# A two-layer graph transformer on one core: layer 1's table weights loaded beside the experts, and a last table tile cut to the nodes' rows

## The chip, the cores and the metric

The kernel runs on one core of a Trainium2 chip. The metric is the device time in microseconds; a shorter time is better. Five engines work from queues of their own: PE (matmul, with its weight loads PEld), DVE (vector), ACT (scalar functions), POOL and SP. In this kernel SP only issues DMAs, and POOL only issues DMAs that gather or scatter rows. All DMAs share the core's 16 DMA engines.

## The reference, cut to what matters

The inputs are 3,125 nodes of 256 features and 100,000 edges with one of 8 types. Two layers follow one another; each adds a graph part, a mixing part and an expert part to the nodes.

```python
xn = _layernorm(x, axis=-1)
x = x + _L0_gnn_ref(xn, edge_index, ...) + _L0_mix_ref(xn[None], ...)[0]
x = x + _L0_ffn_ref(_layernorm(x, axis=-1)[None], ...)[0]        # 8 experts, the best 2 per node
xn = _layernorm(x, axis=-1)
x = x + _L1_gnn_ref(xn, L1_gnn_W, ..., edge_type_8) + _L1_mix_ref(xn[None], ...)[0]
x = x + _L1_ffn_ref(_layernorm(x, axis=-1)[None], ...)[0]
```

What lies around the change is the end of layer 0 and the start of layer 1's graph part:

```python
out = (weights[:, :, None] * sel).sum(axis=1)                    # layer 0: two experts' results per node
...
h_all = jnp.einsum('nf,rof->rno', x, W).reshape(r, n, h, d)      # layer 1: 8 types x 3125 nodes x 256
h_src = h_all[edge_type, src]                                    # one row per edge
scores = einsum(h_src, attn_src) + einsum(h_dst, attn_dst)       # then a softmax over each node's edges
out = jax.ops.segment_sum(h_src * w[..., None], dst, num_segments=n)
```

The layer-1 mixing part needs k and v of all nodes (with a norm of their own), their product kv, and the weights wq, wk, wv, wo and bo.

## The kernel before, in words

The nodes are padded to 25 tiles of 128 (`NB = 25`, `NP = 3200`). The last tile holds only `LAST = 53` nodes; the other 75 of its rows belong to no node. The node features stay on the chip in `xs`.

**The experts (layer 0).** `experts` runs 32 steps of 256 rows (8 fixed, 24 by a plan), over which `s` counts. A step loads the rows (`fx`), small vectors and two halves of an expert's weights (`fw1`, `fw2`, 1 MB each) on SP, two steps of buffers ahead; PE makes the hidden values (`fhp`, line 2068), ACT their Gelu, PE the results (`fyp`, line 2076), DVE adds a bias, and ACT's queue stores the result to `route_y` in DRAM (line 2079). Then `beside(s)` is called, which places other small work next to the step: block lists for layer 1, and the attention's score weights at steps 16 and 22. Here PE, DVE and ACT run in the written order (`manual_schedule` with `ORDERED`); the order of SP and POOL is found by the framework's scheduler, except for what `keep_in_program_order` marks.

**The table stage (layer 1).** After the experts come ten weight loads on SP (lines 353 and 2321 to 2328: `wq`, `wo`, `wt`, `wkv`, `bo`, `kg`, `kb`), and then a loop over the 25 tiles. For a tile POOL gathers the two expert results of each node from `route_y` (`y0`, `y1`, three buffers each, line 2342), DVE adds them to `xs` and takes the norm, PE transposes (`xt1`), and PE multiplies with `wt` for all 8 types (`hp`, line 2362), with `score_w` for the attention's terms (`ap`) and with `wkv` for k and v (`kvp`). ACT and DVE copy the results to `stage`, and SP stores the stage into the table `tab2` in DRAM (line 2375):

```python
rows = tab2[:R * NP, :].rearrange("(r t p) c -> t p r c", r=R, p=P)
...
nc.sync.dma_start(rows[t], stage)         # 128 partitions x 8 types x 264 floats (1,056 bytes a piece)
```

SP also stores the tile's own attention terms (`apart`) and its transposed features (`x1t`). In this loop the scheduler orders all engines.

**The attention blocks (layer 1).** `Layer1.run` is in written order again. POOL gathers one table row per edge, 128 at a time, into the buffers `r` (nine buffers of seven gathers, line 1403); block 0 has 34 of them. A gather reads the whole of `tab2`, so the first waits for every store of it. Beside them SP loads `oe` (line 1207), PE picks each edge's own node terms (`dp`, line 1228), DVE reduces them (`own`, line 1239), and `mix` prepares the mixing weights, before `block` begins with `raw` (line 1422). 25 blocks follow, and out's rows are stored at the end (line 1383; the last store has 53 rows).

Of the kernel before, what the change touches and what calls it, by code (L numbers as in the profile page):

```python
# [8 lines left out]
F32 = mybir.dt.float32  # L9
BF = mybir.dt.bfloat16  # L10
I32 = mybir.dt.int32
AF = mybir.ActivationFunctionType
# [31 lines left out]
def row_bc(v, n, start=0):  # L44

    return bass.AP(tensor=v.tensor, offset=v.offset + start, ap=[[0, P], [1, n]])
# [1962 lines left out]
        nc.vector.tensor_copy(self.back, rank)  # L2009


def experts(tc, C, T, a, pool, wp, wk, ps, beside):

    nc = tc.nc
# [98 lines left out]
def fast(ctx: ExitStack, tc: tile.TileContext, a, out, flag):  # L2113
# [151 lines left out]
    big.close()  # L2265
    late = ctx.enter_context(tc.tile_pool(name="late", bufs=1))


    with tc.tile_pool(name="blk", bufs=1) as blk, tc.tile_pool(name="blk_p", bufs=1, space=PSUM) as blk_p, \
            tc.tile_pool(name="f", bufs=1) as f:  # L2270
        B_ = Blocks(nc, late, dram, blk, a, places)

        score_w = None
        wn = f.tile([P, R, 2, D], F32, name="wn")
# [34 lines left out]
    with tc.tile_pool(name="n1", bufs=1) as n1:  # L2309
        apart = dram.tile([NB, P, 3, HD * R], BF, name="apart")  # L2310
        x1t = dram.tile([(NB + 3) // 4, P, 2, 512], F32, name="x1t")
        cx = n1.tile([P, 2, P], F32, name="cx1")
        wq = load_k(nc, n1, a["L1_mix_wqT"], "wq")
        wo = load_k(nc, n1, a["L1_mix_woT"], "wo")
        with tc.tile_pool(name="r", bufs=1) as r1, tc.tile_pool(name="rw", bufs=3) as rw, \
                tc.tile_pool(name="rc", bufs=1, space=PSUM) as rc, \
                tc.tile_pool(name="rp", bufs=2, space=PSUM) as rp:
# [6 lines left out]
            kg = r1.tile([P, 2, 64], F32, name="kg")  # L2324
            kb = r1.tile([P, 2, 64], F32, name="kb")
            for i, c in enumerate("kv"):
                nc.sync.dma_start(kg[:, i, :], row_bc(a[f"L1_mix_ln_{c}_g"], 64))
                nc.sync.dma_start(kb[:, i, :], row_bc(a[f"L1_mix_ln_{c}_b"], 64))
            pad = r1.tile([1, TW], F32, name="pad")
            nc.vector.memset(pad[:, :D], 0.0)  # L2330
            nc.vector.memset(pad[:, D:], FAR)
            nc.sync.dma_start(tab2[PADTAB:PADTAB + 1, :], pad)

            st = r1.tile([P, NB, 6], F32, name="st_x2")
            mv = r1.tile([P, NB, 2], F32, name="mv_x2")
            rs = r1.tile([P, NB], F32, name="rs_x2")
            cps = [rc.tile([P, P], F32, name=f"kv{g}") for g in range(2)]
            rows = tab2[:R * NP, :].rearrange("(r t p) c -> t p r c", r=R, p=P)
            for t in range(NB):
                for i in range(2):  # L2340
                    y = rw.tile([P, D], F32, name=f"y{i}")
                    nc.gpsimd.indirect_dma_start(  # L2342
                        out=y, out_offset=None, in_=T_.y,
                        in_offset=bass.IndirectOffsetOnAxis(ap=T_.back[:, i * NB + t:i * NB + t + 1], axis=0))
                    nc.vector.scalar_tensor_tensor(xs[:, t, :], y, T_.wt[:, i, t:t + 1], xs[:, t, :],
                                                   op0=OP.mult, op1=OP.add)
                nc.vector.bn_stats(st[:, t, :], xs[:, t, :])
                nc.vector.bn_aggr(mv[:, t, :], st[:, t, :])
                nc.scalar.activation(rs[:, t:t + 1], mv[:, t, 1:2], AF.Sqrt, bias=C.eps)
                nc.vector.reciprocal(rs[:, t:t + 1], rs[:, t:t + 1])  # L2350
                x1 = rw.tile([P, D], F32, name="x1")
                normal(nc, x1, xs[:, t, :], mv, rs, t)
                nc.vector.tensor_add(xs[:, t, :], xs[:, t, :], bo)
                xt = rw.tile([P, 2, P], F32, name="xt1")
                transposed(nc, C, rp, xt, x1)
                nc.sync.dma_start(x1t[t // 4][:, :, t % 4 * P:(t % 4 + 1) * P], xt)

                stage = rw.tile([P, R, TW], F32, name="stage")
                for j in range(R // 2):
                    hp = rp.tile([P, 2, D], F32, name="hp", tag="a")  # L2360
                    for k in range(2):
                        nc.tensor.matmul(hp.rearrange("p r d -> p (r d)"), xt[:, k, :],  # L2362
                                         wt[:, k, j * 512:(j + 1) * 512], start=(k == 0), stop=(k == 1))
                    if j % 2:
                        nc.vector.tensor_copy(stage[:, 2 * j:2 * j + 2, :D], hp)
                    else:
                        nc.scalar.copy(stage[:, 2 * j:2 * j + 2, :D], hp)
                ap = rp.tile([P, 2 * R * HD], F32, name="ap", tag="b")
                for k in range(2):
                    nc.tensor.matmul(ap, xt[:, k, :], score_w[:, k, :], start=(k == 0), stop=(k == 1))  # L2370
                nc.vector.tensor_copy(stage[:, :, D:], ap[:, :R * HD].rearrange("p (r h) -> p r h", r=R))
                a3 = rw.tile([P, 3, HD * R], BF, name="a3")
                bf_parts(nc, rw, a3[:, 0, :], a3[:, 1, :], a3[:, 2, :], ap[:, R * HD:], [P, HD * R])
                nc.sync.dma_start(apart[t], a3)
                nc.sync.dma_start(rows[t], stage)

                n = P if t < NB - 1 else LAST
                kvp = rp.tile([P, 8, 64], F32, name="kvp", tag="b")
                for k in range(2):
                    nc.tensor.matmul(kvp.rearrange("p h d -> p (h d)"), xt[:, k, :], wkv[:, k, :],  # L2380
                                     start=(k == 0), stop=(k == 1))
                mean = rw.tile([P, 8], F32, name="mean")
                nc.vector.tensor_reduce(mean, kvp, AX.X, OP.add)
                nc.vector.tensor_scalar(mean, mean, 1.0 / 64, None, op0=OP.mult)
                kv = rw.tile([P, 8, 64], F32, name="kv")
                nc.vector.tensor_tensor(kv, kvp, mean[:, :, None].to_broadcast([P, 8, 64]), OP.subtract)
                sq = rw.tile([P, 8, 64], F32, name="sq")
                nc.scalar.activation(sq, kv, AF.Square)
                var = rw.tile([P, 8], F32, name="var")
                nc.vector.tensor_reduce(var, sq, AX.X, OP.add)  # L2390
                nc.scalar.activation(var, var, AF.Sqrt, bias=C.eps, scale=1.0 / 64)
                nc.vector.reciprocal(var, var)
                nc.vector.tensor_tensor(kv, kv, var[:, :, None].to_broadcast([P, 8, 64]), OP.mult)
                kv4 = kv.rearrange("p (i h) d -> p i h d", i=2)
                nc.vector.tensor_tensor(kv4, kv4, kg[:, :, None, :].to_broadcast([P, 2, 4, 64]), OP.mult)
                nc.vector.tensor_tensor(kv4, kv4, kb[:, :, None, :].to_broadcast([P, 2, 4, 64]), OP.add)
                kvf = kv.rearrange("p h d -> p (h d)")
                for g in range(2):
                    nc.tensor.matmul(cps[g], kvf[:n, g * P:(g + 1) * P], kvf[:n, D + g * P:D + (g + 1) * P],
                                     start=(t == 0), stop=(t == NB - 1))  # L2400
            for g in range(2):
                nc.vector.scalar_tensor_tensor(cx[:, g, :], cps[g], 1.0 / N, C.blocks[64],
                                               op0=OP.mult, op1=OP.mult)


        with tc.tile_pool(name="at_1", bufs=1) as one, tc.tile_pool(name="at_w", bufs=2) as wk, \
                tc.tile_pool(name="at_r", bufs=9) as rows, tc.tile_pool(name="at_p", bufs=1, space=PSUM) as ps:
            with tc.manual_schedule():
                Layer1(tc, C, a, out, one, wk, rows, ps, B_, tab2, apart, x1t, (cx, wq, wo), xs).run()


@with_exitstack
# [58 lines left out]
```

## Time and profile before

| | |
|---|---|
| median of 3 runs | 3045.12 us (3043.67 to 3058.38) |
| the profiled execution's own time | 3573.77 us |
| its span, from the first instruction to the last | 3571.6 us |
| granted TensorE clock, mean | 0.864 |
| PE, DVE, ACT, POOL busy in the span | 2645.9, 1843.1, 741.6, 990.8 us |
| experts' last result, first `hp` of the table stage | 1415.5, 1435.06 us |
| last store of the table, first gather from it | 1697.17, 1702.80 us |

The profiled execution takes longer than the others; its durations are used for what an instruction costs, and the median for the time. Starts are counted from the beginning of the span. In a line of the timeline stand the start, the duration, the engine (SPq and ACTq are the queues that issue DMAs), the source line, the operation, the names written and read, the shapes, the number merged into the line, and in brackets the idle time before it with what ended it. A wait for several semaphores is put down to the one that came last by the profile, which need not be the one that counted. In a table of stretches, "DMA share" is the mean busy share of the 16 DMA engines.

### The profile page before, as it was taken

What the parts mean: (1) busy time and instruction counts of PE and PEld (TensorE: products, weight loads), DVE (VectorE), ACT (ScalarE), POOL (GpSimd) and SP (SyncE); (2) the same over time, 40 slices, a digit from 0 to 9 for tenths busy, and PEclk for the clock granted to TensorE, in tenths of its full rate; (3) what the DMA queues carried; (4) which work ended last, traced back from release to release, by engine and by line L of the source; (5) the groups of instructions that cost most, each with busy time, mean ns of one, the idle gap of its engine ahead of it and who ended that gap; (6) DMA issues with size and microseconds to landing.
All of it is one profiled execution on the core that took longest, in us unless ns stands there. A gap on an engine that the chain in (4) does not pass through costs nothing.

```text
span 3571.6 us, 38056 instructions
## 1 busy us (share of the span) xinstructions
PE 2645.9 (74%) x13443; PEld 1791.6 (50%) x13485; DVE 1843.1 (52%) x4089; ACT 741.6 (21%) x1662; POOL 990.8 (28%) x1040
## 2 busy tenths in 40 slices
PE   3787999999699998899053557757656747756778
PEld 2555545546588887444043434534444534444456
DVE  7997977565311111866145444545545454454452
ACT  3443111222222222322001011111101111111122
POOL 1000000012360000400634553354444534544500
PEclk9999999999799999899576777778877878877889
DMA  3333565332566655533423333243333433343312
GB/s 98 81 73 88 164 211 165 99 104 74 160 201 203 196 161 175 156 126 128 128 79 83 97 110 103 81 114 104 106 98 101 117 90 92 100 121 87 107 57 84
DMA packets 388220, 421.79 MB, mean 118 GB/s; under 512 B 144181, under 2 KB 322618, under 8 KB 387764
## 3 DMA queue, kind: packets, MB, share of 16 engines
q1 hardware_dynamic: 317486, 270.75, 25.3%
q0 software_dynamic: 49072, 132.49, 13.4%
q10 hardware_dynamic: 21462, 16.03, 1.5%
q8 instruction: 108, 1.77, 0.2%
q14 instruction: 92, 0.75, 0.1%
HBM read 321.17 MB, written 97.96 MB: 117 GB/s over the span
## 4 chain that ended last, share of the span: by engine, by line
PE 50%; DVE 18%; another core or an unknown queue 17%; issue 6%; DMA 5%; ACT 3%; POOL 1%; ACTq 1%; SPq 0%; DVEq 0%; POOLq 0%
PE agg L2218 8%; PE fyp L2076 6%; PE fhp L2068 6%; PE sums L1492 6%; PE hp L1284 5%; PE hp L2362 4%; PE yp L1336 3%; DVE r L1478 2%; DVE oh_a L1656 2%; PE hp L2240 1%; DVE oh_s L1656 1%; DMA at<-adj 1%; PE kv L1764 1%; PE cnt L1671 1%
## 5 line engine op out<-in xcount | busy, mean ns | idle before, releaser
L1403 POOL DMA_INDIRECT r<-tab,b_at x831 | 795.4, 957 | 1101.5 <-ACT xt L1550 447.2
L1492 PE MATMUL sums<-r,oh 128*128 128x264 f32 x1662 | 459.3, 434 | 99.5 <-DVE oh L1481 41.3
L1492 PEld LDWEIGHTS sums<-r,oh 128*128 128x128 f32 x1662 | 355.8, 217 | 194.9 <-issue 87.9
L1228 PE MATMUL dp<-a,ot 128*128 128x64 bf16 x2493 | 118.1, 211 | 351.6 <-DVE own L1239 128.2
L1239 DVE TENSOR_TENSOR own<-dp,orel 128x512 f32<-128x512 f32 (+1 forms) x122 | 74.2, 608 | 490.6 <-remote 338.1
L1228 PEld LDWEIGHTS <-ot 128*128 128x128 bf16 x2493 | 109.2, 110 | 382.8 <-issue 202.1
L1947 POOL DMA_INDIRECT route_x<-x,slot x50 | 50.6, 1012 | 819.7 <-DVE slot L1943 646.3
L1478 DVE TENSOR_TENSOR r<-r,fixed 128x1792 f32<-128x1792 f32 (+2 forms) x123 | 239.5, 1947 | 3.4 <-ACT fixed L1466 3.4
L2068 PE MATMUL fhp<-fxe,fw 128*128 128x256 f32 x1024 | 234.0, 386 | 8.3 <-ACT fhid L2069 7.6
L1336 PE MATMUL yp<-ew,h 128*128 128x256 f32 x600 | 174.4, 443 | 85.6 <-DVE xs L1340 68.7
L1287 ACT ACTIVATE h<-hp,bc 128x512 f32<-128x512 f32 (+2 forms) x168 | 104.9, 639 | 635.5 <-remote 312.6
L2076 PE MATMUL fyp<-fw,fhid 128*128 128x256 f32 x1024 | 226.3, 379 | 0.0
L2218 PE MATMUL agg<-at,py 128*128 128x512 bf16 (+5 forms) x1181 | 215.1, 333 | 2.6 <-issue 1.8
L2218 PE MATMUL agg<-at,px 128*128 128x512 bf16 (+2 forms) x1027 | 213.9, 356 | 1.2 <-DMA row_b<-in_L_gnn_b 0.2
L2068 PEld LDWEIGHTS fhp<-fxe,fw 128*128 128x128 f32 x1024 | 186.9, 192 | 49.4 <-ACT fhid L2069 15.5
L1284 PE MATMUL hp<-xt,ew 128*128 128x512 f32 (+2 forms) x336 | 183.5, 677 | 30.0 <-ACT h L1287 24.6
L2076 PEld LDWEIGHTS fyp<-fw,fhid 128*128 128x128 f32 x1024 | 192.1, 190 | 24.8
L2362 PE MATMUL hp<-wt,xt 128*128 128x512 f32 x400 | 184.6, 610 | 11.1 <-issue 4.4
L1336 PEld LDWEIGHTS yp<-ew,h 128*128 128x128 f32 x600 | 128.7, 223 | 124.8 <-DVE xs L1340 75.1
L2069 ACT ACTIVATE fhid<-fhp,fb 128x256 f32<-128x256 f32 x256 | 120.6, 474 | 299.1 <-PE fhp L2068 221.0
L1284 PE MATMUL hp<-h,ew 128*128 128x512 f32 (+2 forms) x336 | 158.6, 599 | 0.0
L2342 POOL DMA_INDIRECT y<-route_y,slot x50 | 50.7, 1014 | 384.6 <-DMA wq<-in_L_mix_wqT 350.2
(422 smaller groups left out, 3843.7 us busy)
## 6 DMA issues: line engine op xcount, KB each, us to landing
fw<-in_L_ffn_W SPq DMA_DIRECT2D x64, 1024.0 KB
ew<-in_L_ffn_expert_w SPq DMA_DIRECT2D x126, 256.0 KB
at<-adj SPq DMA_DIRECT2D x44, 640.0 KB
route_x<-zero SPq DMA_DIRECT2D x104, 256.0 KB
tab<-stage SPq DMA_DIRECT2D x25, 1056.0 KB
oe<-b_order SPq DMA_DIRECT2D x97, 256.0 KB
adj<-adj_o SPq DMA_DIRECT2D x78, 250.0 KB
r<-tab,b_at POOLq DMA_INDIRECT x831
```

Of the source, the lines that this page charges most:

```text
L1228: nc.tensor.matmul(dp[:, i, :, :].rearrange("p h r -> p (h r)"), ot[:, i * P:(i + 1) * P], A["a3"][:, j, :], start=(j == 0), stop=(j == 2))
L1284: nc.tensor.matmul(hp[:, :W], ws[i, e][:, n, j * P:(j + 1) * P], x[:, n, :W], start=(n == 0), stop=(n == 1))
L1336: nc.tensor.matmul(yp, h2[e][:, n, i * P:(i + 1) * P], ws[3, e][:, n, :], start=(n == 0), stop=(n == 1))
L1403: st = self.nc.gpsimd.indirect_dma_start(out=r[:, c, :], out_offset=None, in_=self.table, in_offset=bass.IndirectOffsetOnAxis(ap=self.B.at ...
L1478: nc.vector.tensor_tensor(rv, rv, self.factors[:, s0:s0 + k, :, None].to_broadcast([P, k, HD, DH]), OP.mult)
L1492: mm = nc.tensor.matmul(self.sums, oh[:, c, :], r[:, c, :], start=(i == 0), stop=(i == w - 1))
L1656: nc.vector.tensor_tensor(oh.rearrange("p w (m two) -> p w m two", two=2), self.row, v[:, :, None, :].to_broadcast(self.shape), OP.is_equal)
L2068: nc.tensor.matmul(hp, w1[:, k, i * P:(i + 1) * P], xe[:, k, :], start=(k == 0), stop=(k == 1))
L2069: nc.scalar.activation(hid[:, i, :], hp, AF.Gelu, bias=b1[:, 0, i:i + 1])
L2076: nc.tensor.matmul(yp, hid[:, i, t * P:(t + 1) * P], w2[:, i, :], start=(i == 0), stop=(i == K1 - 1))
L2218: nc.tensor.matmul(agg[g][:, :cw], parts[j][:n, k, g * P:(g + 1) * P], at[:n, i, :cw], start=(k == 0 and j == 0), stop=(k == NB - 1 and j ...
L2362: nc.tensor.matmul(hp.rearrange("p r d -> p (r d)"), xt[:, k, :], wt[:, k, j * 512:(j + 1) * 512], start=(k == 0), stop=(k == 1))
```

## The change

The loads of the table stage move into a new generator, `table_weights`. Its tiles lie in two memory pools that are opened ahead of the experts' (`n1`, `r`), so they have places of their own. `beside(s)` takes one step of the generator from `s = 24` on: four steps load a quarter of `wt` each, the fifth `wkv` and `bo`, the sixth `kg`, `kb`, `wq` and `wo`. All go through SP, in program order. After the experts ACT takes one square root of a constant.

In the tile loop, the last tile stores only its first 53 rows, the nodes'. The other 75 rows of the last tile's place in the table, which belong to no node but have to hold finite numbers, are stored one tile earlier, out of tile 23's stage. Beyond that the loop's body is moved out by one level and otherwise unchanged.

```diff
+def table_weights(tc, a, n1, r1):
+    nc = tc.nc
+    wq, wo = (n1.tile([P, 2, D], F32, name=n) for n in ("wq", "wo"))
+    wt = r1.tile([P, 2, R * D], F32, name="wt")
+    wkv = r1.tile([P, 2, 2 * D], F32, name="wkv")
+    bo = r1.tile([P, D], F32, name="bo")
+    kg, kb = (r1.tile([P, 2, 64], F32, name=n) for n in ("kg", "kb"))
+
+    def loads():
+        split = lambda name: a[name].rearrange("(k p) n -> p k n", p=P)
+        keep = lambda o, i: tc.keep_in_program_order(nc.sync.dma_start(o, i))
+        for x in range(0, R * D, 512):
+            keep(wt[:, :, x:x + 512], split("L1_gnn_WT")[:, :, x:x + 512])
+            yield
+        for i, name in enumerate(("L1_mix_wkT", "L1_mix_wvT")):
+            keep(wkv[:, :, i * D:(i + 1) * D], split(name))
+        keep(bo, row_bc(a["L1_mix_bo"], D))
+        yield
+        for i, c in enumerate("kv"):
+            keep(kg[:, i, :], row_bc(a[f"L1_mix_ln_{c}_g"], 64))
+            keep(kb[:, i, :], row_bc(a[f"L1_mix_ln_{c}_b"], 64))
+        keep(wq, split("L1_mix_wqT"))
+        keep(wo, split("L1_mix_woT"))
+        yield
+
+    return (wq, wo, wt, wkv, bo, kg, kb), loads()
...
+    n1 = ctx.enter_context(tc.tile_pool(name="n1", bufs=1))
+    table_hold = ExitStack()
+    r1 = table_hold.enter_context(tc.tile_pool(name="r", bufs=1))
...
+        ready = table_weights(tc, a, n1, r1)
...
+            if s >= 24:
+                next(ready[1], None)
...
                 experts(tc, C, T_, a, f, fw, fk, fp, beside)
+                nc.scalar.activation(r1.tile([P, 1], F32, name="root"), C.eps, AF.Sqrt)
...
-        wq = load_k(nc, n1, a["L1_mix_wqT"], "wq")
-        wo = load_k(nc, n1, a["L1_mix_woT"], "wo")
...
-            wt = load_k(nc, r1, a["L1_gnn_WT"], "wt")
-            wkv = r1.tile([P, 2, 2 * D], F32, name="wkv")
-            for i, name in enumerate(("L1_mix_wkT", "L1_mix_wvT")):
-                nc.sync.dma_start(wkv[:, :, i * D:(i + 1) * D], a[name].rearrange("(k p) n -> p k n", p=P))
-            bo = r1.tile([P, D], F32, name="bo")
-            nc.sync.dma_start(bo, row_bc(a["L1_mix_bo"], D))
...
+    wq, wo, wt, wkv, bo, kg, kb = ready[0]
...
-                nc.sync.dma_start(rows[t], stage)
-
-                n = P if t < NB - 1 else LAST
+            n = P if t < NB - 1 else LAST
+            nc.sync.dma_start(rows[t][:n], stage[:n])
+            if t == NB - 2:
+                nc.sync.dma_start(rows[NB - 1][LAST:], stage[LAST:])
...
+    table_hold.close()
```

More of the change, by code (lines that the diff above doesn't have):

```diff
@@ L2306, in fast @@
                 experts(tc, C, T_, a, f, fw, fk, fp, beside)
[L2309 to L2312, printed above, removed]
-        wq = load_k(nc, n1, a["L1_mix_wqT"], "wq")
-        wo = load_k(nc, n1, a["L1_mix_woT"], "wo")
-        with tc.tile_pool(name="r", bufs=1) as r1, tc.tile_pool(name="rw", bufs=3) as rw, \
-                tc.tile_pool(name="rc", bufs=1, space=PSUM) as rc, \
-                tc.tile_pool(name="rp", bufs=2, space=PSUM) as rp:
-            wt = load_k(nc, r1, a["L1_gnn_WT"], "wt")
-            wkv = r1.tile([P, 2, 2 * D], F32, name="wkv")
-            for i, name in enumerate(("L1_mix_wkT", "L1_mix_wvT")):
-                nc.sync.dma_start(wkv[:, :, i * D:(i + 1) * D], a[name].rearrange("(k p) n -> p k n", p=P))
-            bo = r1.tile([P, D], F32, name="bo")
-            nc.sync.dma_start(bo, row_bc(a["L1_mix_bo"], D))
[L2324 to L2368, printed above, removed]
-                for k in range(2):
[L2370 to L2375, printed above, removed]
-                n = P if t < NB - 1 else LAST
[L2378 to L2400, printed above, removed]
-            for g in range(2):
[L2402 to L2409, printed above, removed]
@@ new lines, in fast @@
+                nc.scalar.activation(r1.tile([P, 1], F32, name="root"), C.eps, AF.Sqrt)
+    apart = dram.tile([NB, P, 3, HD * R], BF, name="apart")
+    x1t = dram.tile([(NB + 3) // 4, P, 2, 512], F32, name="x1t")
+    cx = n1.tile([P, 2, P], F32, name="cx1")
+    wq, wo, wt, wkv, bo, kg, kb = ready[0]
+    with tc.tile_pool(name="rw", bufs=3) as rw, tc.tile_pool(name="rc", bufs=1, space=PSUM) as rc, \
+            tc.tile_pool(name="rp", bufs=2, space=PSUM) as rp:
+        pad = r1.tile([1, TW], F32, name="pad")
+        nc.vector.memset(pad[:, :D], 0.0)
+        nc.vector.memset(pad[:, D:], FAR)
+        nc.sync.dma_start(tab2[PADTAB:PADTAB + 1, :], pad)
+        st = r1.tile([P, NB, 6], F32, name="st_x2")
+        mv = r1.tile([P, NB, 2], F32, name="mv_x2")
+        rs = r1.tile([P, NB], F32, name="rs_x2")
+        cps = [rc.tile([P, P], F32, name=f"kv{g}") for g in range(2)]
+        rows = tab2[:R * NP, :].rearrange("(r t p) c -> t p r c", r=R, p=P)
+        for t in range(NB):
+            for i in range(2):
+                y = rw.tile([P, D], F32, name=f"y{i}")
+                nc.gpsimd.indirect_dma_start(
+                    out=y, out_offset=None, in_=T_.y,
+                    in_offset=bass.IndirectOffsetOnAxis(ap=T_.back[:, i * NB + t:i * NB + t + 1], axis=0))
+                nc.vector.scalar_tensor_tensor(xs[:, t, :], y, T_.wt[:, i, t:t + 1], xs[:, t, :],
+                                               op0=OP.mult, op1=OP.add)
+            nc.vector.bn_stats(st[:, t, :], xs[:, t, :])
+            nc.vector.bn_aggr(mv[:, t, :], st[:, t, :])
+            nc.scalar.activation(rs[:, t:t + 1], mv[:, t, 1:2], AF.Sqrt, bias=C.eps)
+            nc.vector.reciprocal(rs[:, t:t + 1], rs[:, t:t + 1])
+            x1 = rw.tile([P, D], F32, name="x1")
+            normal(nc, x1, xs[:, t, :], mv, rs, t)
+            nc.vector.tensor_add(xs[:, t, :], xs[:, t, :], bo)
+            xt = rw.tile([P, 2, P], F32, name="xt1")
+            transposed(nc, C, rp, xt, x1)
+            nc.sync.dma_start(x1t[t // 4][:, :, t % 4 * P:(t % 4 + 1) * P], xt)
+            stage = rw.tile([P, R, TW], F32, name="stage")
+            for j in range(R // 2):
+                hp = rp.tile([P, 2, D], F32, name="hp", tag="a")
+                for k in range(2):
+                    nc.tensor.matmul(hp.rearrange("p r d -> p (r d)"), xt[:, k, :],
+                                     wt[:, k, j * 512:(j + 1) * 512], start=(k == 0), stop=(k == 1))
+                if j % 2:
+                    nc.vector.tensor_copy(stage[:, 2 * j:2 * j + 2, :D], hp)
+                else:
+                    nc.scalar.copy(stage[:, 2 * j:2 * j + 2, :D], hp)
+            ap = rp.tile([P, 2 * R * HD], F32, name="ap", tag="b")
+            for k in range(2):
+                nc.tensor.matmul(ap, xt[:, k, :], score_w[:, k, :], start=(k == 0), stop=(k == 1))
+            nc.vector.tensor_copy(stage[:, :, D:], ap[:, :R * HD].rearrange("p (r h) -> p r h", r=R))
+            a3 = rw.tile([P, 3, HD * R], BF, name="a3")
+            bf_parts(nc, rw, a3[:, 0, :], a3[:, 1, :], a3[:, 2, :], ap[:, R * HD:], [P, HD * R])
+            nc.sync.dma_start(apart[t], a3)
+            n = P if t < NB - 1 else LAST
+            nc.sync.dma_start(rows[t][:n], stage[:n])
+            if t == NB - 2:
+                nc.sync.dma_start(rows[NB - 1][LAST:], stage[LAST:])
+            kvp = rp.tile([P, 8, 64], F32, name="kvp", tag="b")
+            for k in range(2):
+                nc.tensor.matmul(kvp.rearrange("p h d -> p (h d)"), xt[:, k, :], wkv[:, k, :],
+                                 start=(k == 0), stop=(k == 1))
+            mean = rw.tile([P, 8], F32, name="mean")
+            nc.vector.tensor_reduce(mean, kvp, AX.X, OP.add)
+            nc.vector.tensor_scalar(mean, mean, 1.0 / 64, None, op0=OP.mult)
+            kv = rw.tile([P, 8, 64], F32, name="kv")
+            nc.vector.tensor_tensor(kv, kvp, mean[:, :, None].to_broadcast([P, 8, 64]), OP.subtract)
+            sq = rw.tile([P, 8, 64], F32, name="sq")
+            nc.scalar.activation(sq, kv, AF.Square)
+            var = rw.tile([P, 8], F32, name="var")
+            nc.vector.tensor_reduce(var, sq, AX.X, OP.add)
+            nc.scalar.activation(var, var, AF.Sqrt, bias=C.eps, scale=1.0 / 64)
+            nc.vector.reciprocal(var, var)
+            nc.vector.tensor_tensor(kv, kv, var[:, :, None].to_broadcast([P, 8, 64]), OP.mult)
+            kv4 = kv.rearrange("p (i h) d -> p i h d", i=2)
+            nc.vector.tensor_tensor(kv4, kv4, kg[:, :, None, :].to_broadcast([P, 2, 4, 64]), OP.mult)
+            nc.vector.tensor_tensor(kv4, kv4, kb[:, :, None, :].to_broadcast([P, 2, 4, 64]), OP.add)
+            kvf = kv.rearrange("p h d -> p (h d)")
+            for g in range(2):
+                nc.tensor.matmul(cps[g], kvf[:n, g * P:(g + 1) * P], kvf[:n, D + g * P:D + (g + 1) * P],
+                                 start=(t == 0), stop=(t == NB - 1))
+        for g in range(2):
+            nc.vector.scalar_tensor_tensor(cx[:, g, :], cps[g], 1.0 / N, C.blocks[64],
+                                           op0=OP.mult, op1=OP.mult)
@@ L2412, in gps_two_layers @@
+    table_hold.close()
+    with tc.tile_pool(name="at_1", bufs=1) as one, tc.tile_pool(name="at_w", bufs=2) as wk, \
+            tc.tile_pool(name="at_r", bufs=9) as rows, tc.tile_pool(name="at_p", bufs=1, space=PSUM) as ps:
+        with tc.manual_schedule():
+            Layer1(tc, C, a, out, one, wk, rows, ps, B_, tab2, apart, x1t, (cx, wq, wo), xs).run()
 @with_exitstack
```

## The prediction

> **What bounds the kernel now.** I read the page first, then two short stretches, because the change touches only the two ends of layer 1's table stage and the last steps of the experts.
>
> ```profile
> span 3571.6 us, 38056 instructions
> ...
> PE 50%; DVE 18%; another core or an unknown queue 17%; issue 6%; DMA 5%; ACT 3%; POOL 1%; ACTq 1%; SPq 0%; DVEq 0%; POOLq 0%
> ```
>
> The chain that ended last runs half on PE; DMA holds 5% of it. So a DMA edit is worth what the two seams give, not a share of the DMA busy time. The first seam, from the experts' last result (1415.5) to the table stage, in the table of stretches:
>
> ```profile
> core 0: us, PE busy (x) PEld busy (x) DVE busy (x) ACT busy (x) POOL busy (x), PEclk, DMA share, GB/s
> 1418.00:1427.00 9.00, 0.00 (x0) 0.00 (x0) 0.15 (x1) 0.00 (x0) 5.80 (x6) 0.50 0.98 352
> 1427.00:1435.00 8.00, 1.09 (x4) 0.70 (x4) 6.25 (x21) 2.54 (x6) 5.74 (x6) 0.50 0.62 188
> ```
>
> PE does nothing for nine microseconds while the DMA engines are full (0.98, 352 GB/s). The timeline says with what:
>
> ```profile
> 1416.92 0.48 SPq L353 DMA_DIRECT2D wt<-in_L_gnn_WT  x1
> ...
> 1418.50 1.02 POOL L2342 DMA_INDIRECT y<-route_y,slot  x1 [350.16 <-DMA wq<-in_L_mix_wqT]
> ...
> 1426.85 0.48 DVE L2345 SCALAR_TENSOR_TENSOR xs<-y,route_w,xs 128x256 f32<-128x256 f32 x1 [10.36 <-DMA wkv<-in_L_mix_wkT]
> 1427.60 0.95 POOL L2342 DMA_INDIRECT y<-route_y,slot  x1 [1.78 <-DVE xs L2345]
> ...
> 1435.06 8.79 PE L2362 MATMUL hp<-wt,xt 128*128 128x512 f32 x16
> ```
>
> The first gather of y is issued at 1418.50 and used at 1426.85, 8.35 us later, since the weights (wt alone is 2 MB) share its engines. The releaser named at 1418.50 is not the real one: that gather needs the experts' last store, issued at 1415.53. From 1490 on the stage is PE's: 204.35 of 207 us busy, 9.96 us a tile.
>
> The second seam is the end of the table:
>
> ```profile
> 1697.17 0.37 SPq L2375 DMA_DIRECT2D tab<-stage  x1
> ...
> 1702.80 0.94 POOL L1403 DMA_INDIRECT r<-tab,b_at  x1 [199.11 <-DMA apart<-a]
> ...
> 1817.46 0.45 DVE L1422 TENSOR_TENSOR raw<-ad,r 128x56 f32<-128x56 f32 x2
> ```
>
> The last store of the table is issued at 1697.17; POOL's first gather from the table waits for it and starts at 1702.80, 5.63 us after. Then 63 gathers follow at 1.25 us each, and block 0 uses the first 34 at 1817.46. How fast the last store is, is therefore what the second half of the change is about, and two stretches of the trace show a store's pace:
>
> ```profile
> core 0: us, PE busy (x) PEld busy (x) DVE busy (x) ACT busy (x) POOL busy (x), PEclk, DMA share, GB/s
> 1698.20:1701.20 3.00, 0.21 (x1) 0.00 (x0) 1.93 (x4) 0.63 (x1) 0.00 (x0) 1.00 1.03 354
> 3567.25:3568.65 1.40, 0.00 (x0) 0.00 (x0) 0.00 (x0) 0.00 (x0) 0.00 (x0) 0.89 0.07 20
> ```
>
> The first is the last table store, 128 partitions: all 16 DMA engines busy, 354 GB/s. The second is the very last store of the kernel, out's last 53 rows (line 1383): a share of 0.07, one engine of sixteen, and 20 GB/s. The change cuts the last table store to exactly such 53 rows.
>
> **The change, part by part.**
>
> *Weights out of the first seam.* Ten loads, 3,328 KB, and 9.1 us of SP's issuing (1415.94 to 1425.08) leave it. The gathers then have the engines for themselves; in the trace one later in the stage (1441.61) lands after 3.52 us at most, others after 2.5 to 3.0. But POOL itself needs 1.25 us per gather: the six that the buffers allow leave at 1418.50 to 1425.82, so the seventh goes at 1426.1 and lands at about 1429.0. In the order of before DVE puts seven xs additions ahead of tile 0's reciprocal; the seventh started at 1432.30. That gives 3.3 us. Lower bound 1.5: POOL's idle 1.78 us less a little, if only its cadence counts. Upper bound 17.7: all 9.4 us from 1435.06 back to about 1425.7 (three POOL steps and the short chain of tile 0), and the 8.3 us that PE idles in 1447 to 1490 (34.68 of 43 busy) as well, if the queues come out in a better order. I take 3.3, the row with the order that is there; DVE's queue is in order and nothing in the diff reorders it by hand.
>
> *The same loads beside the experts.* They become 13 loads on SP in steps 24 to 29: 512 KB a step for four, then 640 KB, then 640 KB in six loads. A step takes 14.35 us on PE (fhp 6.96 + fyp 6.91 and the transposes). Its own traffic is 2,688 KB, 7.8 us at 352 GB/s; 512 to 640 KB more are 1.5 to 1.9 us. SP issues seven DMAs of about 0.36 us in a step, so it has room; they stand behind fetch's loads, which wait for PE, and the next step's fetch stands behind them. A half of an expert's weights is issued about 21 us ahead of its use (1322.14, landed in under 5 us), so I put 0. If that cover were gone: 3,328 KB at 352 GB/s, 9.7 us. Not below zero: nothing in those steps waits for these bytes.
>
> *The square root's table ahead.* One ACTIVATE on ACT after the last Gelu moves a 1.28 us table load (1429.50) to 1416, where ACT is idle until 1429.50. Its result was not awaited: DVE's reciprocal stood behind the addition of 1432.30. 0, at best 1.3.
>
> *75 of tile 24's 128 rows stored early,* from tile 23's stage: one more SP issue (0.4 us) and 600 pieces of 1,056 bytes, beside a PE-bound tile. 75 splits over fifteen engines, 40 pieces each, 2 us: hidden, 0. On one engine it would be 600 x 49.7 ns = 29.8 us, and the store after it would queue behind it; the trace's 125-row stores (adj, line 1673), which raise their semaphore by five late steps and eleven at once, speak for the split.
>
> *The 53 rows that come last.* 53 x 8 = 424 pieces of 1,056 bytes, 447,744 bytes. Before: 1,024 pieces on 16 engines, 64 each, in 3.18 us (49.7 ns a piece); the issue took 0.90 us to the first packet, and 0.54 us passed from the last one to the landing: 4.62 us in all. The rule that speaks against this edit is the Trainium skill's, page "DMA: Bandwidth & Descriptors", section "Why a DMA increments its semaphore by 16 and not by 1": a transfer gets the largest number of engines up to 16 that divides the slowest dimension of both sides; 127 partitions get one. 53 is prime. The trace agrees: the 53-row load of at at 419.75 raises its semaphore by fifteen within 0.52 us and by the last step only after 6.62 us, and the last row of the table above has one engine. That page's figure for an engine (Specifications), about 27 GiB/s, would give 15.4 us for these bytes. The trace's paces give more: 424 x 49.7 ns = 21.1 us at the table store's own pace, 18.5 us at the 42.5 ns per KB of the tail of out's store, 22.4 us at that store's 20 GB/s. I take 21.1, the same piece in the same direction. Landing after 0.90 + 21.1 + 0.54 = 22.5 us, 17.9 later than before (15.3 and 19.2 by the other two paces, 12.2 by the skill's figure). Net by the skill's figure 12.2 - 3.3 = +8.9; by the trace 17.9 - 3.3 = +14.6. The trace decides.
>
> *Who waits for it.* All 63 gathers of POOL stand behind the first. On SP's queue the store of apart, the small expert biases and the oe loads of block 0 (first one 1708.50) follow on the same engine's ring, so oe lands 10 us or more later too. In the profile DVE's own waits (58.15 us, to 1788.24) end only with the last gather, so the shift passes whole. If these long waits are the profiler's, block 0 starts with the later of the 34th gather (1702.80 + 34 x 1.25 + 3 = 1748) and PE's chain from oe (1713.1 + 4 x 3.36 + 1.5 + 13.6 + 7 = 1748.6): a tie, and after the change the gathers end it. No later block gives it back: each waits for the one before.
>
> **Sum.** 0 + 0 + 0 - 3.3 + 17.9 = +14.6 against the profiled execution's 3573.77, which is 528.65 above the median of the runs, 3045.12. Issue and DMA pace don't hang on that difference, so I carry it over unscaled: 3059.7. What a measurement of this kernel can tell from no change is about 0.5%, 15.2 us; this lies just below.
>
> **Rivals.**
> - *The single engine is slower still.* Its first packets in out's store came at 100 ns; with 60 ns a piece the store takes 25.4 us, +22.2, and with the least start gain, 1.5: +20.7, 3065.8. It decides from 47 ns a piece with that gain, 51 ns with 3.3. For it: 20 GB/s over the 1.4 us. Against it: 42.5 ns in the tail.
> - *The start swallows it (the other side).* PE starts nine microseconds earlier and the idle of 1447 to 1490 goes too: -17.7 + 17.9, 3045.3. From a start gain of 17.9 on it is no slower. For it: PE idle 17.9 us before its first transpose. Against it: POOL's cadence.
> - *The 53 rows are spread after all,* as the change means it: 26.5 pieces an engine, 1.3 us, -1.9; with 3.3 that is 3039.9, with 17.7 it is 3025.5. Against it: every 53-row transfer in the trace.
>
> **Chances.** Likeliest, one engine at 45 to 55 ns and a start gain of 2 to 6: 0.55, own range 3053 to 3067, about half of it (0.27) beyond +15.2, 0.28 within. Slower engine: 0.20, all slower. Start swallows: 0.15, of it 0.10 within, 0.03 faster, 0.02 slower. Spread: 0.10, of it 0.04 within, 0.06 faster. Together slower 0.49, within 0.42, faster 0.09. The range 3032 to 3070 leaves out about a tenth on each side.
>
> **What would show it.** Right: one DMA engine's share (0.06 to 0.07) in the 20 us after the last tab store, POOL's first table gather about 23 us after that issue instead of 5.63, oe late; the gathers of y landing in 3 us, hp's first matmul at about 16 us after the last fy instead of 19.6; experts' steps still 14.35 us. Wrong: a first gather within 6 us of the last table store, a table stage shorter by over 10 us, or experts' steps grown.

## The result, and the profile after

| | before | changed |
|---|---|---|
| median of 21 runs each | 3054.45 us (3043.67 to 3062.43) | 3069.71 us (3059.19 to 3078.62) |
| ratio, 95% interval | | 1.0044 [1.0033, 1.0056] |

The changed kernel is 13.4 us slower (0.0044 x 3054.45; 10.1 to 17.1 by the interval); the prediction's sum was +14.6. The two medians lie 15.3 us apart; the ratio, which comes with an interval, is what is used below. Over 21 runs the median of before is 9.3 us above that of the three runs that were shown, so the absolute forecast of 3059.7 lies 10 us low.

One later set of runs, the kernel before included, lay near 3571 us like the profiled execution behind the prediction, and all the others near 3050 us, so the changed kernel is compared here with a profile of the unchanged one at 3055.95 us (experiment 1).

The page of the changed kernel, its span and the chain that ended last, and then the same chain of the unchanged kernel in experiment 1:

```profile
span 3068.9 us, 38103 instructions
...
PE 60%; DVE 17%; DMA 8%; POOL 7%; issue 5%; ACT 2%; SPq 0%; DVEq 0%; ACTq 0%; POOLq 0%
```

```profile
PE 61%; DVE 17%; DMA 8%; POOL 7%; issue 4%; ACT 2%; SPq 0%; DVEq 0%; ACTq 0%; POOLq 0%
```

The 17% of "another core or an unknown queue" that stood in the prediction's profile are gone from both, and POOL has 7% of both where it had 1%. So these shares show the other execution and not the change; the change is seen only at the seams.

First seam. The last fy (here and below the end of PE's last `fyp` matmul) is at 1404.73. Two stretches at the same distance from it as in the table of before:

```profile
core 0: us, PE busy (x) PEld busy (x) DVE busy (x) ACT busy (x) POOL busy (x), PEclk, DMA share, GB/s
1407.69:1416.69 9.00, 0.00 (x0) 0.00 (x0) 3.02 (x9) 0.29 (x1) 6.50 (x7) 0.50 0.28 81
1416.69:1424.69 8.00, 6.67 (x9) 2.79 (x10) 7.09 (x25) 2.14 (x6) 5.90 (x7) 0.51 0.43 122
```

The DMA share fell from 0.98 to 0.28 (352 to 81 GB/s): the weights are gone from here. PE still does nothing in the first stretch, but in the second it is busy for 6.67 us instead of 1.09. The timeline:

```profile
1408.36 1.01 POOL L2366 DMA_INDIRECT y<-route_y,slot  x1 [348.97 <-issue]
...
1411.63 0.48 DVE L2369 SCALAR_TENSOR_TENSOR xs<-y,route_w,xs 128x256 f32<-128x256 f32 x1 [5.84 <-DMA y<-route_y,slot]
...
1415.48 0.16 DVE L2374 RECIPROCAL rs_x<-rs_x 128x1 f32<-128x1 f32 x1
...
1418.68 8.34 PE L2386 MATMUL hp<-wt,xt 128*128 128x512 f32 x12 [0.89 <-ACT xt L346]
```

The first gather of y is used 3.27 us after its issue, before it was 8.35. hp starts 13.95 us after the last fy; the profile of before in experiment 1 has 19.88.

Second seam, the end of the table (timeline, then a stretch inside the last store):

```profile
1672.72 0.24 SPq L2400 DMA_DIRECT2D tab<-stage  x1
1673.77 14.91 SPq L2398 DMA_DIRECT2D apart<-a  x1
1688.78 0.34 SPq L1173 DMA_DIRECT2D b<-in_L_ffn_expert_b  x1
...
1695.70 0.94 POOL L1403 DMA_INDIRECT r<-tab,b_at  x1 [212.29 <-DMA bc<-in_L_ffn_expert_b1c]
...
1696.71 0.33 SPq L1207 DMA_DIRECT2D oe<-b_order  x1
```

```profile
core 0: us, PE busy (x) PEld busy (x) DVE busy (x) ACT busy (x) POOL busy (x), PEclk, DMA share, GB/s
1675.00:1678.00 3.00, 0.00 (x0) 0.00 (x0) 1.81 (x5) 0.93 (x2) 0.00 (x0) 0.86 0.07 23
```

POOL's first gather comes 22.98 us after the issue of the last store; before it was 5.63 (5.62 in experiment 1). A share of 0.07 is one engine of sixteen. The 424 pieces run from 1673.54 to 1694.35, 49.1 ns each, and the store raises its semaphore for the last time 22.20 us after its issue. SP's next issue, the store of apart, took 14.91 us instead of 0.32, and oe is loaded 13 us later than before, counted from the last store (23.99 us instead of 10.75).

The chain of waits of this stretch shows who stands behind it:

```profile
1689.17 6.30 DMA bc<-in_L_ffn_expert_b1c
1695.70 0.94 POOL r L1403
1696.94 0.95 POOL r L1403
1698.19 0.95 POOL r L1403
...
1735.73 0.95 POOL r L1403
1736.98 4.34 DMA r<-tab,b_at
1741.64 0.63 DVE sc L1425
```

As the cause it names a small load (bc) that landed at about the same time; the gather reads tab, whose last landing is 1672.72 + 22.20 = 1694.92. The load itself was held up by the store: fifteen of its sixteen semaphore steps came by 1690.78, the last only at 1695.48, just behind the store's. From 1695.70 on the 34 gathers of POOL that block 0 needs follow in the chain at 1.25 us each, and DVE's last `raw` of block 0, just ahead of the `sc` in the chain, waits for the landing of the last:

```profile
1741.39 0.21 DVE L1422 TENSOR_TENSOR raw<-ad,r 128x48 f32<-128x48 f32 x1 [2.30 <-DMA r<-tab,b_at]
```

### The profile page after: what moved, and what is told of

It is laid out like the page before. It is cut to its first block, busy times and chain, and to the rows that moved or that the text cites. A ratio compares the mean times of both kernels' runs of the same rounds, so it can differ in the third digit from the quotient of the medians.

```text
span 3068.9 us, 38103 instructions
## 1 busy us (share of the span) xinstructions
PE 2552.3 (83%) x13485; PEld 1745.6 (57%) x13485; DVE 1845.2 (60%) x4089; ACT 744.5 (24%) x1663; POOL 994.9 (32%) x1040
## 4 chain that ended last, share of the span: by engine, by line
PE 60%; DVE 17%; DMA 8%; POOL 7%; issue 5%; ACT 2%; SPq 0%; DVEq 0%; ACTq 0%; POOLq 0%
PE agg L2247 9%; PE sums L1492 8%; PE fhp L2097 7%; PE fyp L2105 7%; POOL r L1403 7%; PE hp L1284 6%; PE hp L2386 6%; PE yp L1336 4%; DMA r<-tab,b_at 3%; DVE oh_a L1656 2%; PE hp L2269 2%; DVE oh_s L1656 2%; DMA at<-adj 1%; PE cnt L1671 1%; PE kv L1764 1%
## 5 line engine op out<-in xcount | busy, mean ns | idle before, releaser
L1492 PE MATMUL sums<-r,oh 128*128 128x264 f32 x1662 | 421.2, 409 | 47.0 <-DVE oh L1481 24.3
L1492 PEld LDWEIGHTS sums<-r,oh 128*128 128x128 f32 x1662 | 332.1, 202 | 129.4 <-issue 30.0
L2247 PE MATMUL agg<-at,py 128*128 128x512 bf16 (+4 forms) x1200 | 217.3, 334 | 0.0
L1336 PE MATMUL yp<-ew,h 128*128 128x256 f32 x600 | 157.9, 413 | 66.7 <-DVE xs L1340 59.6
L1228 PE MATMUL dp<-a,ot 128*128 128x64 bf16 x2493 | 110.6, 207 | 98.3 <-DVE own L1239 43.7
L1284 PE MATMUL hp<-xt,ew 128*128 128x512 f32 (+2 forms) x336 | 165.3, 620 | 23.4 <-ACT h L1287 13.5
L1336 PEld LDWEIGHTS yp<-ew,h 128*128 128x128 f32 x600 | 119.2, 207 | 100.5 <-DVE xs L1340 65.3
L2366 POOL DMA_INDIRECT y<-route_y,slot x50 | 49.1, 983 | 374.9 <-issue 352.9
L2247 PEld LDWEIGHTS <-py 128*128 128x128 bf16 (+1 forms) x1200 | 111.5, 99 | 87.7 <-issue 5.6
L2082 DVE TENSOR_SCALAR fxe<-ftp,flng,flnb 128x256 f32<-128x256 f32 x64 | 31.9, 540 | 210.9 <-PE ftp L2080 175.9
```

Of the source, the lines that this page charges most:

```text
L1228: nc.tensor.matmul(dp[:, i, :, :].rearrange("p h r -> p (h r)"), ot[:, i * P:(i + 1) * P], A["a3"][:, j, :], start=(j == 0), stop=(j == 2))
L1284: nc.tensor.matmul(hp[:, :W], ws[i, e][:, n, j * P:(j + 1) * P], x[:, n, :W], start=(n == 0), stop=(n == 1))
L1336: nc.tensor.matmul(yp, h2[e][:, n, i * P:(i + 1) * P], ws[3, e][:, n, :], start=(n == 0), stop=(n == 1))
L1492: mm = nc.tensor.matmul(self.sums, oh[:, c, :], r[:, c, :], start=(i == 0), stop=(i == w - 1))
L2247: nc.tensor.matmul(agg[g][:, :cw], parts[j][:n, k, g * P:(g + 1) * P], at[:n, i, :cw], start=(k == 0 and j == 0), stop=(k == NB - 1 and j ...
```

## Experiments

Three lengths are read from each profile: from the end of the last fy to the first hp of the table stage (A), from there to the last issue of a store into tab (B), from there to the first gather from tab (C). A + B + C is the way that the change touches, but for the experts' steps beside which the weights are now loaded. In the experiments each ratio is to runs of the kernel before on the same chip; they lay on three chips.

| kernel | A | B | C | sum, against before | ratio to before [95%] |
|---|---|---|---|---|---|
| before, again | 19.88 | 255.63 | 5.62 | 281.1 | 0.9996 [0.9982, 1.0010] |
| changed | 13.95 | 254.04 | 22.98 | 291.0, +9.8 | 1.0044 [1.0033, 1.0056] |
| whole last store | 13.96 | 254.09 | 5.44 | 273.5, -7.6 | 0.9984 [0.9972, 0.9996] |
| split alone | 20.19 | 255.52 | 23.18 | 298.9, +17.8 | 1.0058 [1.0040, 1.0075] |
| 64 rows last | 13.94 | 253.40 | 5.41 | 272.8, -8.4 | 0.9979 [0.9966, 0.9993] |
| 58 rows last | 13.97 | 253.84 | 13.84 | 281.7, +0.5 | 1.0024 [1.0012, 1.0037] |
| 48 and 5 rows last | 13.94 | 255.42 | 4.12 | 273.5, -7.6 | 0.9978 [0.9964, 0.9991] |
| whole, no square root | 16.61 | 257.68 | 5.44 | 279.7, -1.4 | 0.9999 [0.9982, 1.0015] |
| whole, late loads | 14.77 | 253.50 | 5.36 | 273.6, -7.5 | 0.9985 [0.9970, 0.9999] |
| 48 and 5, late loads | 14.25 | 255.39 | 4.07 | 273.7, -7.4 | 0.9999 [0.9985, 1.0014] |
| 53 rows on POOL's queue | 13.94 | 257.10 | 29.08 | 300.1, +19.0 | 1.0086 [1.0068, 1.0105] |

**1. The kernel before, again.** No edit.

> The kernel before, unchanged, for a profile of it that stands to its median. Ratio 1.000 by every theory. Theory A (the parts of the prediction's sum, read in a profile 528 us longer than the median, are the ordinary ones): last fy to first hp of the table stage about 19.6 us, first hp to last tab store about 262 us, last tab store to first table gather 5.6 us. Theory B (that profile ran its table stage slower than an ordinary execution does): the stretch from first hp to last tab store is near the changed kernel's 254.0 us here, so that little was gained in it, and the start's gain is the 6.0 us in the stretch before hp alone.

Theory B holds: B is 255.63 us here, not 262.1.

```profile
1421.41 1.22 PE L2362 MATMUL hp<-wt,xt 128*128 128x512 f32 x1
...
1677.03 0.37 SPq L2375 DMA_DIRECT2D tab<-stage  x1
...
1682.66 0.94 POOL L1403 DMA_INDIRECT r<-tab,b_at  x1 [199.13 <-DMA apart<-a]
```

Of the 6.5 us that the profile behind the prediction had more, nothing was there to gain in an execution of 3055 us. The change brought 5.9 us in A and 1.6 in B.

**2. The last store whole again: the early weights and the square root alone.**

```diff
-            nc.sync.dma_start(rows[t][:n], stage[:n])
-            if t == NB - 2:
-                nc.sync.dma_start(rows[NB - 1][LAST:], stage[LAST:])
+            nc.sync.dma_start(rows[t], stage)
```

> The changed kernel, but the last table tile is stored whole with one transfer of 128 rows: the early weights and the early square root alone. Theory A (the parts add up; the 53-row store costs 17.4 us, which is the first gather at 22.98 us after the last store instead of 5.63): 17 us below the changed kernel, so 3 to 5 us below the kernel before, ratio 0.9984 to 0.9990. Rival 1 (the start really gains the 14.1 us that the two traces show from the last fy to the last tab store, and the 53-row store costs more in the blocks than its 17.4): ratio about 0.9954. Rival 2 (the loads cost PE time beside the experts): ratio 1.000 or above, and experts' steps longer than in the kernel before by 0.3 us or more.

Ratio 0.9984, 4.9 us below before; C is 5.44 again. Theory A. The seam shows 7.6 us; rival 1's 0.9954 is outside the interval. Of rival 2 a little is there: five of the steps beside which weights are loaded take 14.38 us instead of 14.31, 0.35 us in all.

**3. The split alone, in the kernel before.**

```diff
-                nc.sync.dma_start(rows[t], stage)
                 n = P if t < NB - 1 else LAST
+                nc.sync.dma_start(rows[t][:n], stage[:n])
+                if t == NB - 2:
+                    nc.sync.dma_start(rows[NB - 1][LAST:], stage[LAST:])
```

> The kernel before with the last table tile cut as in the change: 53 rows last, 75 rows out of tile 23's stage; the weights stay where they were. Theory A (one DMA engine carries the 53 rows, and nothing hides it): first table gather 22 to 23 us after the last tab store instead of 5.6, the time 17 us above the kernel before, ratio 1.0057. Rival 1 (the blocks have slack at their start and give part back): first gather as late, ratio below 1.0030. Rival 2 (the early weights, not the split, made the changed kernel slower): ratio 1.000.

Ratio 1.0058, 17.7 us (0.0058 x 3055.89), and C grew by 17.56 us. Theory A: nothing is given back.

**4. How many rows come last.** Three kernels change nothing but the number of rows, or the number of transfers. The first has 64 rows; the second has 58 where 64 stands here:

```diff
             n = P if t < NB - 1 else LAST
-            nc.sync.dma_start(rows[t][:n], stage[:n])
+            m = P if t < NB - 1 else 64
+            nc.sync.dma_start(rows[t][:m], stage[:m])
             if t == NB - 2:
-                nc.sync.dma_start(rows[NB - 1][LAST:], stage[LAST:])
+                nc.sync.dma_start(rows[NB - 1][64:], stage[64:])
```

> The changed kernel, but 64 rows of the last tile come last and the other 64 of its place are stored early: more bytes last, 512 pieces instead of 424. Theory A (the count of rows sets the count of engines; 64 divides over 16): 32 pieces an engine at 49.7 ns, 1.6 us, landing about 3.0 us after the issue and the first table gather about 4.0 us after it; the time about 19 us below the changed kernel and 1 to 2 us below the whole store, ratio to before about 0.998. Rival (the cost lies in the bytes or in a partial tile, not in the number 53): as slow as the changed kernel or slower, ratio 1.0044 or more, first gather 23 us or later.

> The changed kernel, but 58 rows of the last tile come last (464 pieces) and 70 are stored early. Theory A (a transfer gets the largest number of engines up to 16 that divides its rows; 58 is 2 x 29, so two): 232 pieces an engine at 49.1 ns, 11.4 us, landing about 12.8 us after the issue and the first table gather about 13.6 us after it; 8.2 us above the whole store, ratio to before about 1.0011. Rival 1 (only a prime number of rows falls to a single engine; others are spread over nearly all): first gather at 5.4 us, ratio 0.998. Rival 2 (any number that 16, 15 or 14 does not divide goes to one engine): 22.8 us of pieces, first gather at 25 us, ratio 1.005.

The third keeps the 53 rows and cuts them in two:

```diff
-            nc.sync.dma_start(rows[t][:n], stage[:n])
+            if t < NB - 1:
+                nc.sync.dma_start(rows[t], stage)
+            else:
+                for lo, hi in ((0, 48), (48, LAST)):
+                    nc.sync.dma_start(rows[t][lo:hi], stage[lo:hi])
```

> The changed kernel with the same 53 rows last, but as two transfers: 48 rows, then 5. Theory A (the number of rows of one transfer sets its engines: 48 on 16, 5 on 5): 24 pieces an engine at the 79 ns of the 64-row store, 1.9 us, and 8 pieces on each of five engines, a second issue of about 0.5 us: first table gather 4.6 to 5.4 us after the first of the two issues, time within 1 us of the whole store, ratio about 0.998, some 18 us below the changed kernel with the same bytes last. Rival (it is the 53 partitions or the bytes that come last, not how they are cut): as late as in the changed kernel, first gather at 23 us, ratio 1.0044.

C is 22.98 us with 53 rows, 13.84 with 58 and 5.41 with 64. The store of 58 rows (2 x 29) raises its semaphore by its last steps at 12.66 and 13.06 us; 12.8 was expected from two engines. A stretch inside that store, and the stretches of the 64-row store and of the whole store:

```profile
core 0: us, PE busy (x) PEld busy (x) DVE busy (x) ACT busy (x) POOL busy (x), PEclk, DMA share, GB/s
1679.00:1682.00 3.00, 0.00 (x0) 0.00 (x0) 1.81 (x5) 0.93 (x2) 0.00 (x0) 0.95 0.13 41
```

```profile
1674.20:1676.20 2.00, 0.00 (x0) 0.00 (x0) 1.43 (x3) 0.41 (x1) 0.00 (x0) 1.00 0.92 194
```

```profile
1673.50:1675.50 2.00, 0.00 (x0) 0.00 (x0) 1.53 (x3) 0.30 (x1) 0.00 (x0) 1.00 1.04 360
```

A share of 0.13 is two engines; 0.92 and 1.04 are all sixteen. The 75 rows that the changed kernel stores early raise their semaphore by fifteen late steps, and the 5 rows of the third kernel by five. So the number of rows sets the engines, by its divisors: it is not the bytes, since more rows (58, 64) are faster than 53, and not only a prime that is slow, since 58 got two engines. The time of the kernel with 58 rows, 7.3 us above before, is more than the 3.4 expected, and the seam shows only +0.5; that difference is open.

Two expectations failed in size. 64 rows were to start the gathers at 4.0 us and did so at 5.41, as late as the whole store: on sixteen engines half the rows moved at 194 GB/s instead of 360 (a piece took 79 ns in the median instead of 49), so the pieces took 3.02 us from first to last, against 3.18. And 48 and 5 rows start the gathers 5.57 us after the first of the two issues, where 4.6 to 5.4 was expected: apart is issued between the two, and the second is issued 1.44 us after the first. The cut thus costs nothing any more, but brings little either. At the same bytes last, 0.9978 stands against the changed kernel's 1.0044.

**5. The square root left out,** from the kernel of experiment 2.

```diff
-                nc.scalar.activation(r1.tile([P, 1], F32, name="root"), C.eps, AF.Sqrt)
```

> The early weights with the last tile stored whole, without the early square root: the weights alone. In its instruction order DVE has seven additions of xs ahead of tile 0's reciprocal, as in the kernel before; with the square root it has four. Theory A (the prediction's 3.3 us is what the freed DMA engines give with seven additions ahead; the rest of the start's gain comes from the order that the square root brought): gathers of y land in about 2.7 us, first hp about 16.4 us after the last fy (kernel before 19.9, with the square root 13.95), so 2 to 3 us above the whole store with the square root, ratio about 0.9990. Rival (the square root is worth only its own table load of 1.28 us or nothing, the weights bring all 5.9): first hp at 14.0 to 15.2 us, ratio 0.9984 to 0.9988.

Theory A, and more clearly than expected. A is 16.61 us (16.4 expected) and B 257.68, the longest in the table: the seam is 6.2 us longer than with the square root, and the time is that of before (0.9999). By time alone the two are not told apart, since the intervals of 0.9984 and 0.9999 overlap. The timeline shows why:

```profile
1415.54 0.29 ACT L2372 ACTIVATE rs_x<-mv_x,eps 128x1 f32<-128x1 f32 x1 [7.51 <-DVE mv_x L2371]
...
1419.94 0.48 DVE L2368 SCALAR_TENSOR_TENSOR xs<-y,route_w,xs 128x256 f32<-128x256 f32 x1 [0.60 <-DMA y<-route_y,slot]
1420.35 0.22 DVE L2373 RECIPROCAL rs_x<-rs_x 128x1 f32<-128x1 f32 x2
...
1422.47 2.93 PE L2385 MATMUL hp<-wt,xt 128*128 128x512 f32 x3
```

ACT has tile 0's root at 1415.83, but DVE takes its reciprocal only at 1420.35, since the additions of xs up to the seventh stand ahead of it in DVE's queue and wait for their gathers. With the square root the framework's scheduler writes another order, with four additions ahead instead of seven, and the reciprocal follows the root's end (1414.58) by 0.90 us. It is not the table load that is saved: without the square root too ACT loads its table at 1406.75, long before it is needed.

```profile
1406.75 1.28 ACT L2372 ACT_TABLE_LOAD   x1 [7.29 <-DVE ok L2332]
```

**6. The loads issued after the experts,** in the kernel of experiment 2.

```diff
-            if s >= 24:
-                next(ready[1], None)
...
+    for _ in ready[1]:
+        pass
     apart = dram.tile([NB, P, 3, HD * R], BF, name="apart")
```

> The early square root with the last tile stored whole, but the 13 loads of the weights are issued after the experts, as in the kernel before: the square root alone. In its instruction order DVE has four additions ahead of tile 0's reciprocal. Theory A (order and weights each give a part): the first gather of y still lands after 7 to 8 us, but the reciprocal needs only the fourth: first hp about 17 us after the last fy, 3 us before that of the kernel before, ratio about 0.9990; experts' steps all 14.31 us. Rival (the weights bring all): first hp at 19 to 20 us, ratio 1.000.

The time fits theory A (0.9985), A does not (14.77 us instead of 17). This kernel does not do what the edit was for: the tiles have places of their own, and SP's order is the scheduler's, so wt, wkv and bo were still issued ahead of the last fy (1405.83):

```profile
1395.10 1.92 SPq L2023 DMA_DIRECT2D wt<-in_L_gnn_WT  x4
...
1408.41 0.34 SPq L2023 DMA_DIRECT2D kg<-in_L_mix_ln_k_g  x1
...
1410.70 0.47 SPq L2023 DMA_DIRECT2D wo<-in_L_mix_woT  x1
```

Only kg, kb, wq and wo, some 0.6 MB, are left at the seam. It shows that a head start of up to eight steps isn't needed, with the experts' steps back at 14.31 us; it doesn't show the square root alone. The square root in the kernel before, its loads where they were, was not tried.

**7. The same with 48 and 5 rows, and both once more on one chip.** The two kernels differ only in when the weights are issued.

> The early square root, the last 53 rows as 48 and 5, and the 13 weight loads after the experts as in the kernel before: nothing of the early loading. Theory A (the early loads are worth nothing once the order of DVE's queue is the good one; the gain is the square root's and the smaller last store's): ratio 0.9975 to 0.9985, first hp about 14.8 us after the last fy, first table gather about 4.1 us after the second of the two issues. Rival (the early loads carry the gain of 6 us in the kernel with 48 and 5 rows): ratio 0.9990 to 1.000.

> The kernel with 48 and 5 rows last, early weights and early square root, once more, beside the one with late weights on the same chip. Theory A (from the last fy to the first table gather both take 273.5 to 273.7 us in their traces, 7.4 us less than the kernel before with its 281.1, so the early loads add nothing to the square root's order): the two ratios lie within 0.0010 of each other, near 0.998. Rival (the early loads are worth what the ratios 0.9978 and 0.9999 of the two calls say): this one 0.002 below the other.

> The same with late weights, on the same chip in the same rounds. Theory A: ratio near 0.998, within 0.0010 of the kernel with early weights. Rival: 0.9995 to 1.0005, about 0.002 above it, although the trace shows the seam as short.

Late loads with 48 and 5 rows gave 0.9999 [0.9985, 1.0014] where the seam is as short as with early loads (273.7 and 273.5 us). The repetition on one chip, in the set of runs near 3571 us, gave 0.9992 [0.9968, 1.0017] with early loads and 1.0005 [0.9977, 1.0033] with late ones. Neither pair tells them apart. So what the early issue is worth beyond the seam, nothing or 0.1 to 0.2%, stays open.

**8. The 53 rows on POOL's queue.**

```diff
-            nc.sync.dma_start(rows[t][:n], stage[:n])
+            (nc.sync if t < NB - 1 else nc.gpsimd).dma_start(rows[t][:n], stage[:n])
```

> The changed kernel with the 53-row store put on POOL's DMA queue instead of SP's, so that SP's store of apart, and the loads of a3 and oe of block 0, need not stand behind it. Theory A (what the late store costs is POOL's row of gathers, which runs without a pause up to block 5; the loads of oe are late beside it and cost nothing more): the first table gather still starts about 23 us after the issue, block 0's raw comes back to about 53 us after the last tab store (changed kernel 64.9), and the time stays at the changed kernel's, ratio 1.0035 to 1.0050. Rival 1 (the late loads of oe and apart make the cost): raw at 53 us and the time with it, ratio about 1.000 although the gathers are late. Rival 2 (POOL's queue cuts the 53 rows over all engines): first gather within 6 us, ratio about 0.998.

Ratio 1.0086 [1.0068, 1.0105], slower than the changed kernel, and none of the three expectations fits. POOL took 3.17 us to issue the store, which fell on one engine again, and the first gather came 29.08 us after (1669.04 to 1698.12). oe did not come early as meant: SP's own queue waits for the store before it issues oe (probably because oe's buffer takes the memory that `stage` had; this was not tried):

```profile
SPq L1207 <- DMA tab<-stage: 12.9, 1, 12.9
```

So this run doesn't separate the gathers from oe. What separates them is a reading of two profiles, of the changed kernel and of the one with the whole store. Counted from the last table store, the last raw of blocks 0 to 4 comes at 54.2, 93.8, 137.1, 180.3 and 223.4 us with the whole store, and at 68.7, 110.2, 153.5, 196.7 and 239.6 us in the changed kernel: 14.5 us later in block 0 and 16.2 to 16.4 in the next four. Block 0's first raw is 12.3 us late (52.6 and 64.9), about as late as oe (13.2), but its last one waits for the gathers, which are 17.5 us late, as the chain above shows. From block 1 on the blocks follow one another at about 43 us in both, near the 42.5 us that POOL needs for 34 gathers of 1.25 us. The reading is that POOL is the bound and passes on what its first gather loses; no run forced this alone.

The lowest ratios seen are those with the early weights, the square root and 64 rows, or 48 and 5, last: 0.9979 and 0.9978. Their intervals overlap with that of the whole store (0.9984).

## Why the prediction was right

*The 53 rows: right in mechanism and size.* Predicted: one engine, 49.7 ns a piece, landing after 22.5 us, +17.9. Measured: one engine (0.07), 49.1 ns, 22.20 us, +17.4 in the profile and +17.7 by the time of experiment 3. The estimate of +12.2 from the Trainium skill's 27 GiB/s for an engine ("DMA: Bandwidth & Descriptors", Specifications) was too low: this store ran at 21.5 GB/s, or 20 GiB/s (447,744 bytes in 20.81 us), and the trace's own piece decided rightly. The rival of a spread over sixteen engines is refuted by the share of 0.07, that of a still slower engine (60 ns) by the 49.1 ns.

*The 75 rows early: right.* The store's landing took 6.35 us, its issue 1.31 us rather than 0.4, and B is the same with and without it (254.04 and 254.09).

*The loads beside the experts: nearly right.* 0 was predicted, 0.35 us measured.

*Weights out of the first seam: right in place, mis-sized in what stays.* The predicted 3.3 us, with seven additions ahead, is what experiment 5 shows in A: 19.88 to 16.61. But 2.05 us of it are given back in B, 1.3 of them at once: in the first 40 us after hp PE idles 5.6 us (34.4 busy), in the kernel before 4.3 (35.7 busy). The seam keeps 1.4 us.

*The square root's table ahead: the step that failed.* It was put at 0, at best 1.3, from the table load that it moves, because DVE's reciprocal stood behind the seventh addition of xs anyway. The sentence "nothing in the diff reorders it by hand" was true and beside the point: one more instruction for the scheduler brought another order of DVE's queue, 2.65 us in A and 3.6 in B. So the whole start gave 7.5 us (5.9 in A, 1.6 in B) where 3.3 was in the sum. The prediction's sign, hp about 16 us after DVE's last fy, came out as 13.5; 16.1 is what the kernel without the square root has.

*The sum.* By the seams it is -7.5 + 17.4 + 0.35 = +10.2; measured 13.4 [10.1, 17.1], predicted 14.6. All three lie within the interval, but that 14.6 came so close is in part luck. The gain at the start was taken 4 us too small, and most of that was made up by something that no seam shows: in time the kernels with the new start stand 1 to 4 us above what their seams say (7 us in those with 58 rows, with 48 and 5 rows and late loads, and with the store on POOL's queue). For this no cause was shown. The prediction also held 15.2 us for the least that can be told from no change; over 21 runs the interval is only some 3.5 us to each side, so 13.4 is clear of it.

*Who waits.* That oe would be 10 us late or more was right (13.2). That the gathers would end block 0 after the change was right too: its last raw waits for the 34th. The load of bc shows why what follows on SP's queue is late as well: the part of it that came last landed just behind the store. The waits of 58 us of DVE, which the prediction had doubted, are absent from the profile of experiment 1.

*The start swallows it.* It needed 17.9 us; 7.5 came, and hp still starts 14 us after the last fy.

## What to carry to other kernels

Before a DMA is trimmed to the rows that count, look at how many rows it has: 53 rows on one engine took 22.2 us where 128 on sixteen took 4.6, and 64 took no longer than 128. Price the last transfer ahead of a long row of gathers at its full landing, since nothing behind it gives the time back. And when a change adds or drops an instruction where a scheduler sets the order, compare the queues of the two builds: here a single unused square root shortened the seam by 6.2 us (experiment 5), and moving 3.3 MB of loads alone shortened it by 1.4.

## What the runs showed of the hardware that was not expected

- Sixteen engines are no promise of speed: from 64 partitions they stored 194 GB/s (pieces of 79 ns in the median), from 128 partitions 360 GB/s (49 ns). Why was not tried.
- Behind a store on few engines the queue is held up at its next issue: SP took for it 14.91 us behind one engine, 6.05 us behind two, 0.33 us behind sixteen. Why was not tried.
- On POOL's queue the same 53 rows went out as 106 packets of 4,224 bytes on one engine, 218 ns each on average, and landed 28.3 us after the issue, later than the 424 pieces of SP's queue (22.2).
